# Kernel groups of the lead in order, and late tables moved beside a running convolution

## The chip, the cores and the metric

The kernel runs on one core of a Trainium2 chip. The metric is the device time of one execution in microseconds (us); each kernel is run several times and the median is given. One execution of each kernel is also recorded by the hardware profiler. Its record is "the profile"; answers to questions put to that record are "the trace".

## The reference

The reference filters an input along its length by a state-space convolution and puts a feed-forward network with 4-bit weights on the result. Cut to what matters:

```python
# per head h (64 heads), N = 64 modes, L = 1024 positions, B = 32 sequences
dt  = exp(log_dt);  A = -exp(log_A_real) + 1j * A_imag
Cs  = C * (exp(A * dt) - 1) / A
K   = 2 * Re( sum_n Cs[h, n] * exp(A[h, n] * dt[h] * l) )      # l = 0 .. 1023
y   = causal_convolution(x * mask, K) + D * x * mask           # mask: l < length of the sequence
y   = y * mask
# feed-forward network over the 1024 positions, weights dequantized from 4 bits, groups of 128
gate, up = y @ Wg, y @ Wu                                      # 1024 -> 2752 each
out = x + (silu(gate) * up) @ Wd                               # 2752 -> 1024
```

Each of the 2048 rows (32 sequences x 64 heads) of 1024 positions is one row of the network's input.

## The kernel before

**Blocks.** The 64 heads form four blocks of 16. A block is 16 heads x 32 sequences = 512 columns. The convolution of a block (`conv(blk)`) yields `xh` and `xl`, the high and low float16 halves of the block's network input. There are two such pairs, `c.x[0]` and `c.x[1]`: blocks 0 and 2 use the first, blocks 1 and 3 the second. The network runs on two blocks at a time.

**From parameters to a convolution.** The 64 heads get their convolution kernels in groups of 4 or 8 heads, named by their first head (0, 4, 8, 16, 24, 32, ...). A group passes these steps:

- decay tables: an exponential on ACT (ScalarE), result `xd` (L168 in the lead, L179 in the wide form for two groups);
- phase tables: eight operations on DVE (VectorE), L192 to L204, then sine and square on ACT, L207 and L209 (`phase_tables`, called by `Core.tables`);
- factors `e2` and `e1`: five operations on DVE, L218 to L223 (`kernel_factors`);
- `make_kernel`: small matmuls on PE (TensorE) into the PSUM tile `kq` (L425, L427), its high and low float16 halves `kb` by ACT and DVE (L430, L431), and two stores of `kb` to the DRAM tensor `kpad` (L433). Groups below 24 are stored from ACT's DMA queue, later ones from SP's.
- `toeplitz`: for each head one 512 KB load that reads `kpad` as a 128-row Toeplitz matrix (L525, on SP's queue). Most heads use the three rotating buffers of the tile `t0`, called `t` in the profile; heads of the first block also use borrowed space in `w` and `ihl`.
- `conv_head`: 24 matmuls (L548), eight generator steps of three; after each pair of heads DVE masks the result (`y`, L560), ACT takes the high half `xh` (L563), and GpSimd, or DVE for the last head of a block, the low half `xl` (L565).

The input `u` of four heads is loaded by SP, cast to `uh` by ACT and split into `ul` by DVE (`conv_load`, L503 to L510; `conv_split` in the lead, L495 and L497).

**The lead.** The code from `load_params` to the first network stage handles the parameters (`head_coefficients`, in pieces run by `section`), groups 0, 4 and 8 and conv(0). While conv(0) steps, the table `events` runs extra work at given step numbers (eight steps per head): the kernels of groups 8 and 16, ratios of the scales (`ratios_gu`), a load, and fillers. A filler (`busy`, L891) multiplies two tables into a PSUM tile that nothing reads.

**The network.** `gu_one` and `gu_pair` make gate and up products (L664, L665 and L687, L688) with a rescale of the PSUM tile `chq` after each of eight groups, on DVE (L618, L637) or ACT (L620, L640). `dn_pair` makes the down product for 256 output rows and one block in 22 steps of four matmuls (L736, L737; the last of two, L741), each followed by a rescale on either engine. It ends with a scaled copy `o` (L754 or L758), a residual load `xr` on SP (L775, `residual`), two adds (L762, one on GpSimd and one on DVE) and two stores (L767, GpSimd's queue). The `xr` tile shares a tag with two buffers with `sg`, the output of silu. Weights are unpacked from 4 bits by DVE, GpSimd and ACT (`unpack`, L578 to L599), the down weights `wd` up to and into stage 3.

**The order.** `roll` runs the chains of the network as generators in turn, up to three at a time in the PSUM place "b". Its stages: 0 and 1, single blocks 0 and 1; 2, pairs for blocks 0 and 1; 3 and 4, down products of blocks 0 and 1; 5, pairs for blocks 2 and 3; 6 and 7, their down products. Side work (`sides`) advances by a rate per chain step: in stages 3 and 4 the generator `convs_it` (conv(2), then conv(3)) at `RATES["convs"]`, 1.9 steps. When the first chain of the next stage is opened, what is left of side work marked True is run to its end. The groups 48 and 56 that conv(3) needs are made by `fourth()`, whose scratch space is `c.x[1]` and a pool opened where the unpacking's buffers had been.

Above this, the tile framework orders instructions of each engine by its own planning. `with self.after(key)` gives a key of `self.marks`, an instruction after which the following ones may be placed. Each engine then executes its list in order. SP's list holds DMA issues, and an issue that waits holds those behind it.

Of the kernel before, what the change touches and what calls it, by code (L numbers as in the profile page):

```python
# [32 lines left out]
RATES = {"first": (0.5, 4.6), "fill": (1.0, 0.8), "third": 0.5, "convs": 1.9}  # L33
# [149 lines left out]
def phase_tables(nc, side, pool, co, cst, h0, nh):  # L183
# [20 lines left out]
    stt(r2, r2, off2, pl[:, :, 32:], ALU.subtract, ALU.subtract)  # L204
# [5 lines left out]
    return r1, r2, sq_op  # L210
# [48 lines left out]
class Core:  # L259
    def __init__(self, ctx, tc, io):  # L260
# [15 lines left out]
        self.kpad = self.dram.tile([H, 2, 1152], F16, name="kpad")  # L276
        self.dm, self.known, self.ready = {}, set(), set()
# [127 lines left out]
    def scale_ratios(self, s16, nt, g, name, last_factor):  # L405
# [4 lines left out]
        nc.scalar.copy(s, s16)  # L410
# [32 lines left out]
    def tables(self, pool, h0, nh):  # L443
        held = h0 >= 24
        steps = phase_tables(self.nc, self.nc.vector, pool, self.co, self.cst, h0, nh)
        while True:
            try:
                with self.after("dve" if held else None), self.after("act" if held else None):
                    next(steps)
            except StopIteration as done:  # L450
                self.tab, sq_op = done.value[:2], done.value[2]
                break
            self.dve(800)
            yield
        self.mark(("sq", h0), sq_op)
        self.act(5000)
        yield
        yield from self.pause(5000)
# [33 lines left out]
    def conv_split(self, k, after, last="e"):  # L492
        u, uh, ul = self.us[k]
        with self.after(("sq", after)):
            self.nc.scalar.copy(uh, u)  # L495
        with self.after((last, after)):
            self.nc.vector.tensor_tensor(ul, u, uh, ALU.subtract)  # L497
        self.us[k] = uh, ul
# [219 lines left out]
    def dn_pair(self, k, blk, place):  # L718
# [31 lines left out]
        xr = self.res[k] if blk == 3 else self.residual(self.fw, 2 * k, blk)  # L750
# [21 lines left out]
    def residual(self, pool, n0, blk):  # L772
        rows, cols = slice(128 * n0, 128 * n0 + 256), slice(512 * blk, 512 * blk + 512)
        xr = pool([128, 2, 512], F32) if callable(pool) else pool.tile([128, 2, 512], F32, name="xr", tag="sg", bufs=2)
# [68 lines left out]
def tile_ssm_ffn(ctx, tc, io):  # L843
# [39 lines left out]
    xd = [decay_tables(nc, kg, co, c.cst, h0) for h0 in (0, 8)]  # L883
# [9 lines left out]
    for k, h0 in enumerate((0, 4)):  # L893
        every(c.tables(tables, h0, 4))
# [4 lines left out]
        busy(h0, 8 - 4 * k)  # L899
        c.conv_split(k, h0)  # L900
    every(c.tables(kg, 8, 8))
    every(c.factors(kg, 8, 8, xd[1]))
    c.masks()
# [23 lines left out]
    def kernel_8():  # L927
        c.make_kernel(kg, 8, 8, "b")
        with c.after("act"):
            xd.extend(decay_tables(nc, kg, co, c.cst, h0) for h0 in (16, 24))  # L930
        for k in (2, 3):
            c.conv_split(k, 8, "kb")
# [10 lines left out]
    events = {7: kernel_8, 63: lambda: busy(4, 10), 56: ratios_gu, 87: load_16, 75: lambda: c.make_kernel(kg, 16, 8, "b")}  # L943
    for i, _ in enumerate(c.conv(0)):
        if i in events:
            with c.after("dve" if i == 56 else None):
# [56 lines left out]
    def fourth():  # L1003
        c.forced = True
        every(third_it)
        c.forced = False
        while not c.ready.issuperset(("dn", k, part) for k in range(4) for part in range(3)):
            yield
        c.up_stack.close()
        with tc.tile_pool(name="kg2", bufs=1, side="right") as kg2:  # L1010
            space = c.x[1]
            yield from c.decays(c.scratch(space[:1]), (48, 56))
            c.taps(kg2, 48)
            for h0 in (48, 56):
                yield from c.tables(ScratchPool(c.scratch(space[1:])), h0, 8)
                yield from c.factors(kg2, h0, 8, c.xds[h0])
                for _ in range(3):
                    yield
                c.make_kernel(kg2, h0, 8, "a")
                yield  # L1020
# [3 lines left out]
    def convs():  # L1024
        yield from c.conv(2)
        c.forced = True
        c.need(*(("dn", k, part) for k in range(4) for part in range(3)))
        every(fourth_it)
        c.forced = False
# [97 lines left out]
```

## Time and profile before

| | us |
|---|---|
| median of 3 runs | 1074.47 (1073.33 to 1075.77) |
| the profiled execution's own time | 1075.33 |
| its span in the profile | 1073.5 |
| PE busy | 1026.2 (96%) |
| DVE busy | 803.7 (75%) |
| ACT busy | 775.6 (72%) |
| GpSimd busy | 246.5 (23%) |

Busy shares are means over the whole span. In the row of slices each digit is a fortieth of the span, 26.8 us; PEclk is the clock that the matmul engine was granted, in tenths. In a timeline row the columns are start, duration, engine, line, operation, tiles and count, and in brackets the idle time before it and what ended that. `<-` stands between output and input.

### The profile page before, as it was taken

The numbers are of one execution on the slowest core, as the hardware profiler recorded it, in microseconds if no ns is written. First come the engines' busy times: TensorE is split into PE (matmuls) and PEld (weight loads), VectorE is DVE, ScalarE is ACT, GpSimd is POOL, SyncE is SP. The second block draws the span as 40 slices with busy tenths as digits, with TensorE's granted clock in tenths as the row PEclk, the third lists the DMA queues.
The fourth block names the chain that finished last, engine by engine and source line by source line (L and its number), as shares of the span: only waits on it lengthen the run. The fifth ranks groups of instructions, "written<-read, shape, count | busy, mean of one in ns | idle before, by whom it ended". The sixth has DMA issues, their size and how long they took to land.

```text
span 1073.5 us, 15382 instructions
## 1 busy us (share of the span) xinstructions
PE 1026.2 (96%) x5854; PEld 513.5 (48%) x5854; DVE 803.7 (75%) x939; ACT 775.6 (72%) x1034; POOL 246.5 (23%) x270
## 2 busy tenths in 40 slices
PE   3989999999999999997999999999999999999996
PEld 2867444444344445663665444444444444444442
DVE  8965788888977786768446777777877777777776
ACT  5767777787677777777577777666666667878775
POOL 0333233232332242231103112221111222102102
PEclk9999999999999999999999999999999999999998
DMA  6976321111111534546753001000000001424102
GB/s 197 331 244 211 101 69 40 40 59 40 42 48 50 143 88 156 164 156 196 231 167 128 30 29 51 20 13 17 20 20 20 20 20 58 129 79 148 59 1 79
DMA packets 52099, 99.76 MB, mean 93 GB/s; under 512 B 9524, under 2 KB 11444, under 8 KB 52024
## 3 DMA queue, kind: packets, MB, share of 16 engines
q1 hardware_dynamic: 38888, 70.09, 20.8%
q0 software_dynamic: 5280, 17.31, 4.3%
q10 hardware_dynamic: 7856, 11.37, 3.6%
q8 instruction: 46, 0.75, 0.3%
q14 instruction: 29, 0.24, 0.1%
HBM read 78.99 MB, written 19.76 MB: 92 GB/s over the span
## 4 chain that ended last, share of the span: by engine, by line
PE 83%; ACT 5%; DMA 4%; DVE 4%; issue 2%; POOL 0%; SPq 0%; DVEq 0%; ACTq 0%
PE chq L687 23%; PE chq L688 22%; PE chq L736 13%; PE chq L737 13%; PE cq L548 6%; PE chq L664 2%; PE chq L665 2%; DMA t<-kpad 2%; ACT chq L640 1%; DVE chq L618 1%; ACT chq L620 1%; DVE v L700 1%; DMA ihl<-kpad 1%; DMA ihl<-xF 1%; PE chq L741 1%
## 5 line engine op out<-in xcount | busy, mean ns | idle before, releaser
L687 PE MATMUL chq<-xh,w 128*128 128x512 f16 x1216 | 460.4, 380 | 5.7 <-DVE chq L618 2.1
L688 PE MATMUL chq<-xl,w 128*128 128x512 f16 x1216 | 458.6, 380 | 0.0
L618 DVE TENSOR_SCALAR chq<-chq,gur 128x1024 f32<-128x1024 f32 x261 | 333.2, 1289 | 95.3 <-PE chq L688 94.1
L620 ACT ACTIVATE chq<-chq,gur 128x1024 f32<-128x1024 f32 x285 | 304.3, 1085 | 86.8 <-PE chq L688 85.5
L640 ACT ACTIVATE chq<-chq,dnr 128x512 f32<-128x512 f32 x372 | 242.1, 661 | 71.7 <-PE chq L737 63.8
L736 PE MATMUL chq<-ihl,wd 128*128 128x512 f16 x672 | 253.8, 380 | 6.5 <-ACT chq L640 3.5
L737 PE MATMUL chq<-ihl,wd 128*128 128x512 f16 x672 | 253.4, 380 | 0.0
L637 DVE TENSOR_TENSOR chq<-chq,dnr 128x1024 f32<-128x1024 f32 x129 | 158.4, 1231 | 83.6 <-PE chq L737 83.2
L688 PEld LDWEIGHTS <-w 128*128 128x128 fp8e4 x1216 | 118.9, 98 | 155.3 <-issue 19.4
L687 PEld LDWEIGHTS <-w 128*128 128x128 fp8e4 x1216 | 118.9, 98 | 145.9 <-issue 1.9
L310 POOL TENSOR_TENSOR ihl<-v,ihl 128x512 f16<-128x512 f32 x42 | 48.3, 1150 | 362.9 <-ACT ihl L629 362.9
L737 PEld LDWEIGHTS <-wd 128*128 128x128 fp8e4 x672 | 65.5, 98 | 76.0 <-issue 12.7
L548 PEld LDWEIGHTS <-t 128*128 128x128 f16 x1152 | 81.4, 98 | 39.2 <-DMA t<-kpad 5.9
L736 PEld LDWEIGHTS <-wd 128*128 128x128 fp8e4 x672 | 65.7, 98 | 67.7 <-issue 1.7
L548 PE MATMUL cq<-uh,t 128*128 128x256 f16 (+3 forms) x720 | 91.8, 226 | 4.6 <-DMA t<-kpad 4.5
L565 POOL TENSOR_TENSOR xl<-y,xh 128x512 f16<-128x512 f32 x28 | 36.2, 1294 | 161.5 <-ACT xh L563 161.5
L548 PE MATMUL cq<-ul,t 128*128 128x256 f16 (+3 forms) x360 | 71.6, 225 | 0.0
L629 ACT CAST ihl<-v 128x512 f16<-128x512 f32 x42 | 25.9, 617 | 58.7 <-DVE v L700 55.3
L700 DVE SCALAR_TENSOR_TENSOR v<-chq,gul,sg 128x1024 f32<-128x1024 f32 x38 | 48.6, 1280 | 17.1 <-PE chq L688 11.3
L310 POOL TENSOR_TENSOR spill<-v,spill 128x512 f16<-128x512 f32 x42 | 48.8, 1161 | 14.2 <-ACT spill L629 13.9
L640 ACT ACTIVATE chq<-chq,gur 128x512 f32<-128x512 f32 x66 | 43.2, 661 | 11.0 <-PE chq L665 9.8
L590 POOL TENSOR_TENSOR w<-w,z 128x256 int32<-128x256 int32 x42 | 31.5, 770 | 82.0 <-DVE w L584 77.6
(250 smaller groups left out, 820.5 us busy)
## 6 DMA issues: line engine op xcount, KB each, us to landing
t<-kpad SPq DMA_DIRECT2D x48, 512.0 KB, 4.4
spill<-spill POOLq DMA_DIRECT2D x42, 256.0 KB, 2.7
ihl<-spill ACTq DMA_DIRECT2D x42, 256.0 KB, 2.8
z<-zc SPq DMA_DIRECT2D x29, 256.0 KB, 3.7
u<-xF SPq DMA_DIRECT2D x12, 512.0 KB, 3.7
xr<-xT SPq DMA_DIRECT2D x12, 512.0 KB, 4.7
out<-xr POOLq DMA_DIRECT2D x24, 256.0 KB, 2.9
w<-qgu SPq DMA_DIRECT2D x21, 256.0 KB, 4.1
```

The costliest lines, as they stand in the source:

```text
L310: self.nc.gpsimd.tensor_tensor(out, a, b, op)
L548: nc.tensor.matmul(q[:, d:, h % 2, :], t0[:, lw, 128 * d:128 * d + 128], uu[:, 0:8 - d, h % 4, :], start=(d == 0 and k == 0 and h % 2 == 0 ...
L565: split.tensor_tensor(xl[:, :, ts], yv, xh[:, :, ts], ALU.subtract)
L618: self.mark("dve", self.nc.vector.tensor_scalar(q, q, col, None, ALU.mult))
L620: self.mark("act", self.nc.scalar.activation(q, q, AF.Copy, scale=col))
L637: self.mark("dve", self.nc.vector.tensor_tensor(q, q, cols.to_broadcast([128, 2, 512]), ALU.mult))
L640: self.mark("act", self.nc.scalar.activation(q[:, k], q[:, k], AF.Copy, scale=cols[:, k]))
L687: nc.tensor.matmul(q[:, b], lw, xh[:, g, :], start=(g == 0), stop=False, skip_group_check=True)
L688: nc.tensor.matmul(q[:, b], lw, xl[:, g, :], start=False, stop=(g == GH - 1), skip_group_check=True)
L700: nc.vector.scalar_tensor_tensor(v, q, last, self.sg.pop(ct - 21), ALU.mult, ALU.mult)
L736: nc.tensor.matmul(qs[j], lw, self.ihl[:, g, 0], start=(g == 0), stop=False, skip_group_check=True)
L737: nc.tensor.matmul(qs[j], lw, self.ihl[:, g, 1], start=False, stop=False, skip_group_check=True)
```

## The change

In the lead, groups are put in a fixed order on DVE: the tables of group 4 come after the factors of group 0, those of group 8 after the tables of group 4. The decay tables of heads 8 to 15 come after the squares of group 0. The input splits 0 and 1 come later, and so do the masks. Fillers become 8, 2 and 6 where there were 8, 4 and 10. In conv(0) the kernel of group 8 moves from step 7 to 23, that of group 16 from 75 to 66, and the gate-up scale ratios from 56 to 72.

Late, `fourth()` no longer waits for the unpacking and no longer opens a pool; all of its scratch lies in `c.x[1]`. `convs()` no longer forces it between conv(2) and conv(3): it yields until group 56 is known, and forces `fourth()` only if the side work is itself forced. The rate of `convs` becomes 1.52. The residual tiles of blocks 0 to 2 get a pool `xrp` of two buffers, opened at the end of the first down chain where the unpacking's pool was.

```diff
-RATES = {"first": (0.5, 4.6), "fill": (1.0, 0.8), "third": 0.5, "convs": 1.9}
+RATES = {"first": (0.5, 4.6), "fill": (1.0, 0.8), "third": 0.5, "convs": 1.52}
...
-    def tables(self, pool, h0, nh):
+    def tables(self, pool, h0, nh, key=None):
...
-                with self.after("dve" if held else None), self.after("act" if held else None):
+                with self.after("dve" if held else key), self.after("act" if held else None):
...
+                self.mark(("r", h0), done.value[3])
...
-        nc.scalar.copy(s, s16)
+        with self.after("act"):
+            nc.scalar.copy(s, s16)
...
-        xr = self.res[k] if blk == 3 else self.residual(self.fw, 2 * k, blk)
+        if blk == 3:
+            xr = self.res[k]
+        else:
+            if self.xrp is None:
+                self.need(*(("dn", j, part) for j in range(4) for part in range(3)))
+                self.up_stack.close()
+                self.xrp = self.up_stack.enter_context(self.tc.tile_pool(name="xrp", bufs=2, side="right"))
+            xr = self.residual(self.xrp, 2 * k, blk)
...
-    xd = [decay_tables(nc, kg, co, c.cst, h0) for h0 in (0, 8)]
+    xd = [decay_tables(nc, kg, co, c.cst, 0)]
...
-    for k, h0 in enumerate((0, 4)):
-        every(c.tables(tables, h0, 4))
+    for h0, fillers in ((0, 8), (4, 2)):
+        every(c.tables(tables, h0, 4, ("e", 0)))
+        if h0 == 0:
+            with c.after(("sq", 0)):
+                xd.append(decay_tables(nc, kg, co, c.cst, 8))
         every(c.factors(kg, h0, 4, xd[0][:, h0:h0 + 4]))
         c.make_kernel(kg, h0, 4, "b")
         for h in range(h0, h0 + 4):
             c.t0[h] = c.toeplitz(h)
-        busy(h0, 8 - 4 * k)
-        c.conv_split(k, h0)
-    every(c.tables(kg, 8, 8))
+        busy(h0, fillers)
+    c.conv_split(0, ("sq", 4), ("e", 4))
+    every(c.tables(kg, 8, 8, ("r", 4)))
+    c.conv_split(1, ("sq", 4), ("r", 8))
     every(c.factors(kg, 8, 8, xd[1]))
-    c.masks()
+    with c.after(("e", 8)):
+        c.masks()
...
-    events = {7: kernel_8, 63: lambda: busy(4, 10), 56: ratios_gu, 87: load_16, 75: lambda: c.make_kernel(kg, 16, 8, "b")}
+    events = {23: kernel_8, 63: lambda: busy(4, 6), 72: ratios_gu, 87: load_16, 66: lambda: c.make_kernel(kg, 16, 8, "b")}
...
     def fourth():
-        c.forced = True
-        every(third_it)
-        c.forced = False
-        while not c.ready.issuperset(("dn", k, part) for k in range(4) for part in range(3)):
+        first, second = c.x[1]
+        yield from c.decays(c.scratch([first[:, :4]]), (48, 56))
+        c.taps(ScratchPool(c.scratch([first[:, 4:6]])), 48)
+        for h0 in (48, 56):
+            small = ScratchPool(c.scratch([first[:, 6:8], second[:, 7:8]]))
+            yield from c.tables(ScratchPool(c.scratch([second[:, :7]])), h0, 8)
+            yield from c.factors(small, h0, 8, c.xds[h0])
+            yield from c.pause(c.td - c.tp + HOP)
+            c.make_kernel(small, h0, 8, "a")
             yield
-        c.up_stack.close()
-        with tc.tile_pool(name="kg2", bufs=1, side="right") as kg2:
-            space = c.x[1]
-            yield from c.decays(c.scratch(space[:1]), (48, 56))
-            c.taps(kg2, 48)
-            for h0 in (48, 56):
-                yield from c.tables(ScratchPool(c.scratch(space[1:])), h0, 8)
-                yield from c.factors(kg2, h0, 8, c.xds[h0])
-                for _ in range(3):
-                    yield
-                c.make_kernel(kg2, h0, 8, "a")
-                yield
...
     def convs():
         yield from c.conv(2)
-        c.forced = True
-        c.need(*(("dn", k, part) for k in range(4) for part in range(3)))
-        every(fourth_it)
-        c.forced = False
+        while 56 not in c.known:
+            if c.forced:
+                next(fourth_it)
+            yield
         yield from c.conv(3)
```

More of the change, by code (lines that the diff above doesn't have):

```diff
@@ L203, in phase_tables @@
     stt(r1, r1, off1, pl, ALU.subtract, ALU.subtract)
-    stt(r2, r2, off2, pl[:, :, 32:], ALU.subtract, ALU.subtract)
+    last = stt(r2, r2, off2, pl[:, :, 32:], ALU.subtract, ALU.subtract)
     yield
@@ L209, in phase_tables @@
         sq_op = nc.scalar.activation(r, r, AF.Square, scale=1.4142135623730951)
-    return r1, r2, sq_op
+    return r1, r2, sq_op, last
 def kernel_factors(nc, pool, co, xd, s1, s2, h0, nh):
@@ L276, in __init__ @@
         self.kpad = self.dram.tile([H, 2, 1152], F16, name="kpad")
+        self.xrp = None
         self.dm, self.known, self.ready = {}, set(), set()
@@ L490, in conv_fetch, with conv_split @@
         self.nc.sync.dma_start(self.raw[k][0], self.io["xF"][k])
-    def conv_split(self, k, after, last="e"):
+    def conv_split(self, k, act, dve):
         u, uh, ul = self.us[k]
-        with self.after(("sq", after)):
+        with self.after(act):
             self.nc.scalar.copy(uh, u)
-        with self.after((last, after)):
+        with self.after(dve):
             self.nc.vector.tensor_tensor(ul, u, uh, ALU.subtract)
@@ L773, in residual @@
         rows, cols = slice(128 * n0, 128 * n0 + 256), slice(512 * blk, 512 * blk + 512)
-        xr = pool([128, 2, 512], F32) if callable(pool) else pool.tile([128, 2, 512], F32, name="xr", tag="sg", bufs=2)
+        xr = pool([128, 2, 512], F32) if callable(pool) else pool.tile([128, 2, 512], F32, name="xr")
         self.nc.sync.dma_start(
@@ L928, in kernel_8 @@
         c.make_kernel(kg, 8, 8, "b")
+        for k in (2, 3):
+            c.conv_split(k, "act", ("kb", 8))
         with c.after("act"):
             xd.extend(decay_tables(nc, kg, co, c.cst, h0) for h0 in (16, 24))
-        for k in (2, 3):
-            c.conv_split(k, 8, "kb")
         steps = c.tables(kg, 16, 8)
@@ L941, in load_16 @@
         c.us[4] = c.conv_load(16)
-    events = {7: kernel_8, 63: lambda: busy(4, 10), 56: ratios_gu, 87: load_16, 75: lambda: c.make_kernel(kg, 16, 8, "b")}
+    events = {23: kernel_8, 63: lambda: busy(4, 6), 72: ratios_gu, 87: load_16, 66: lambda: c.make_kernel(kg, 16, 8, "b")}
     for i, _ in enumerate(c.conv(0)):
         if i in events:
-            with c.after("dve" if i == 56 else None):
+            with c.after("dve" if i == 72 else None):
                 events[i]()
```

## The prediction

> **What bounds the kernel now.** I read the page's busy shares and 40 slices first, then tables of engine busy time by stretch, then the timelines of the stretches in which the matmul engine is not full.
>
> ```profile
> PE 1026.2 (96%) x5854; PEld 513.5 (48%) x5854; DVE 803.7 (75%) x939; ACT 775.6 (72%) x1034; POOL 246.5 (23%) x270
> ...
> PE   3989999999999999997999999999999999999996
> ...
> PEclk9999999999999999999999999999999999999998
> ```
>
> TensorE sets the end: 1026 of 1073.5 us. A gain can only come from its idle time, its fillers and its half-clock time. Besides the two ends of the program, the 19th slice (a 7, from 483 us) is the hole. The table by stretch gives both places that the diff touches (columns: length, then busy time and count of PE, PE weight load, DVE, ACT, POOL; last the clock, DMA share, GB/s):
>
> ```profile
> 28.00:30.00 2.00, 1.26 (x20) 1.10 (x21) 1.85 (x4) 1.99 (x7) 0.00 (x0) 0.89 0.18 53
> 30.00:32.00 2.00, 2.00 (x19) 1.88 (x17) 1.44 (x2) 1.95 (x5) 0.00 (x0) 0.50 0.88 215
> 32.00:34.00 2.00, 2.00 (x30) 1.78 (x28) 1.78 (x3) 1.14 (x4) 0.26 (x1) 0.76 1.01 277
> ...
> 490.00:520.00 30.00, 22.14 (x175) 12.47 (x174) 18.50 (x34) 18.10 (x33) 1.15 (x1) 0.94 0.67 211
> 520.00:580.00 60.00, 60.00 (x486) 36.88 (x485) 31.68 (x29) 46.08 (x72) 11.56 (x11) 1.00 0.54 167
> ```
>
> 490 to 520 us: 7.9 us idle. The 3 us stretches inside have clocks 0.86 (495 to 498) and 0.57 (498 to 501): 3 x 0.14 + 3 x 0.43 = 1.7 us more. So 9.6 us lie there. In the lead the clock halves after a gap: 0.2 + 1.0 + 0.5 = 1.7 us. The timelines name the waits:
>
> ```profile
> 17.53 0.63 PE L427 MATMUL kq<-e2t,e1t 128*32 128x32 f32 x8 [13.60 <-DVE e1t L223]
> 18.09 3.78 PE L891 MATMUL wq<-e2t,e1t 128*128 128x128 f32 x16
> ...
> 28.73 0.69 PE L427 MATMUL kq<-e2t,e1t 128*32 128x32 f32 x16 [1.97 <-DVE e1t L223]
> 29.36 12.48 PE L548 MATMUL cq<-ihl,w 128*128 128x256 f16 x168
> 41.69 2.48 PE L891 MATMUL wq<-e2t,e1t 128*128 128x128 f32 x20
> ...
> 60.31 0.28 PE L548 MATMUL cq<-uh,t 128*128 128x256 f16 x1 [1.85 <-DMA t<-kpad]
> ```
>
> The lead is one chain, repeated per group of heads: DVE tables, ACT sine and square, DVE factors, `kq` on PE, `kb` on ACT and DVE, a store to `kpad`, a Toeplitz load, convolution. PE also executes in order, so `kq` of group 8 (28.73) holds seven ready heads behind it.
>
> **The change part by part.**
>
> *Late tables.* Before, `fourth()` waits until all of `wd` is unpacked and is then forced between conv(2) and conv(3): tables, factors, kernels and loads of groups 48 and 56 stand bare. After, it starts in the idle half of `x` with stage 3 and runs beside conv(2); in the built order both `kq` stand among down-projection matmuls with convolutions on both sides, and conv(3) follows without a break. The whole 9.6 us is recovered. No operation is added: two table loads, one wide exponential and two groups of tables as before. Two things are charged back.
>
> (a) Rate 1.9 becomes 1.52 convolution steps per down-projection step. In the built order, before, three quarters of a head remained when the next stage was opened; now 8 heads (192 matmuls, 8 x 1.7 = 13.6 us) stand nearly alone: four heads, 7 others, three heads, 5 others, one head. They live on three `t` buffers.
>
> ```profile
> 510.55 0.28 PE L548 MATMUL cq<-uh,t 128*128 128x256 f16 x1 [1.51 <-DMA t<-kpad]
> ...
> 512.27 14.63 SPq L525 DMA_DIRECT2D t<-kpad  x5
> ...
> 517.04 0.28 PE L548 MATMUL cq<-uh,t 128*128 128x256 f16 x1 [0.84 <-DMA t<-kpad]
> ```
>
> That is the same pattern: head 48 ends at 512.2, its buffer is reloaded at 512.27, head 51 starts at 517.04, a turnaround of 4.8 us. Two other heads cover 3.4. In the new block: heads 56 to 58 are loaded, head 59 waits 1.4 us; the 7 others (7 x 0.216 = 1.5 us) then restore the lead for 60 to 62; head 63 waits about 0.3. At the end stage 5 needs the last head's `y`, `xh`, `xl` (0.2 + 0.69 + 0.62 + 0.69 = 2.2 us) against 4 + 2 + 1 matmuls of cover (1.5 us): 0.7. Sum 2.4; between 0 (loads land early) and 5.
>
> (b) The table work now competes with rescales. The nearest row is the same two-group work of `third()` among the pairs at 228 to 292 us: PE idle in the 4 us stretches there sums to 3.4 us, and the clock fell to 0.69 and 0.88 (1.7 us), so 5.1 us. The pairs have no convolution to fill in; the new order puts 13 to 18 convolution matmuls (about 1 us) where it meets the tables. Bounds 0 and 5.1; I take 2.5, the middle.
>
> Late part: 9.6 - 2.4 - 2.5 = 4.7 us.
>
> *Residual buffers.* `xr` gets two buffers of its own instead of sharing `sg`. SP executes in order: the third and later `xr` loads wait for an earlier store (add, then 2.9 us to land, some 6 us after that chain's last matmul), and `t` loads of heads 57 to 59, 60 to 62 and 63 stand behind such waits in the built order. The chains end about 13, 3 and 2.4 us before the block, so the releases come at about -7, +3 and +4 us on the block's clock; the loads behind could go at 0, 3.4 and 11.4. Cost 0; if a store slips by 3 us, head 60 is late by 2.
>
> *Lead.* Before the first `e1`, DVE no longer has L192, L194, L197, L198, L200, L201, L203, L204 of group 4 and L192 of group 8. By start-to-start that is 0.34 + 0.34 + 0.26 + 0.20 + 0.33 + 0.20 + 0.39 + 0.26 + 0.60 = 2.9 us; part of it filled gaps between dependent coefficient steps (about 0.2 us each when nothing lies between), so I take 2.1: first `kq` at 15.4 instead of 17.5. The rest does not follow. ACT now runs Exp, Sine, Exp, Sine where it ran Exp, Sine: two more table loads, and the second decay table (8 x 0.245 = 2.0 us) stands before `kb` of group 0. Walking the built order with the durations of before: squares of group 0 end 13.1, load and decays 16.4, `kb` 16.7, its store 17.5, sine load 18.8, squares of group 4 at 19.9. DVE has five group-8 steps in front (until 20.3), then factors of group 4 end at 22.3 (before: 20.8). Eight fillers end at 19.8, so PE now waits some 2 us for group 4, then `kq` and two fillers: head 0 at 23.6 instead of 24.5.
>
> Here a rule speaks against the change. The Trainium skill ("ScalarE: Activation LUTs", sections on table sets and the cost of a table load) says to finish one function set before switching and to budget about 2.7 us for each switch, drain included. The row:
>
> ```profile
> 37.91 1.28 ACT L207 ACT_TABLE_LOAD   x1
> 39.20 0.94 ACT L207 ACTIVATE r<-r 128x512 f32<-128x512 f32 x2
> ```
>
> The next activation starts 1.29 us after the load. By the page the two loads would put group 4's factors at about 25 and head 0 at 26.3, 1.8 us later than before; by the row 0.9 earlier. I take the row.
>
> After head 0 the gain is this: `kq` of group 8 now stands behind three heads, so PE no longer waits 1.97 us for it. But the new 2 us gap before group 4 is of the size that halved the clock at 29. The skill ("TensorE: Matmul & The Clock Gate", section on why this matters) allows gaps up to about 3 us. By the page no half clock: 1.7 us more. By the row it returns at 23 to 26. Then `kq` of group 8 comes at 30 to 31, not 28.7, and the loads of group 8 some 1 us later. They were hidden by 2.48 us of fillers at 41.7; six fillers stay. Group 16 gains: its `kb` waited behind two L596 casts (47.20 to 49.28 us), one of which moves behind it (1.1 us). The scale ratios, a mask and two splits move off DVE and ACT at no cost, since the first rescale is at 64.2. So the first head of block 1 (60.31, bound by its load) gains 0.8 with the half clock and 2.0 without. I take 1.3; bounds -1.8 and 3.
>
> *Sum.* 4.7 + 1.3 = 6.0 us. The profiled execution took 1075.33 (span 1073.5, 1.8 around it), which becomes 1069.3; it was 0.86 above the median of the runs, so 1074.47 - 6.0 = 1068.5.
>
> **The rivals.**
>
> *All of it is had* (loads lead, tables hide among convolutions): late part 9.6 - 1.0, lead 2.0, so 1063.9. For it: DMA share at 520 to 580 is 0.54, and PE has convolutions in stage 3. Against: 228 to 292.
>
> *The late part only moves its stall.* With (a) 4 and (b) 5.1 it pays 0.5, lead 1.3: 1072.7. For it: DVE and ACT are already 70 to 75% busy at 405 to 490, with eight unpackings still to come.
>
> *Slower: the block of eight heads starves.* In the lead the same Toeplitz loads landed in 8.2 us at the median, with DMA share above 1.0; at 490 to 610 they landed in 4.4. If the block, where loads go back to back beside `xr` and `spill` loads, takes 8.2, each three heads take 1.7 + 8.2 = 9.9 instead of 5.1: (a) is 8/3 x 4.8 = 12.8 us, and the sum 9.6 - 12.8 - 2.5 + 1.3 = -4.4: 1078.9. It decides from a landing of 6.5 us up. Against: one head per 2.2 us asks for only 240 GB/s, and 417 were seen in the lead.
>
> *It does nothing:* not possible in this built order, since both `kq` and their tables left the stall.
>
> **How the numbers follow.** Likeliest 0.62 (own range 1065.5 to 1071.5), all of it 0.17, moved stall 0.10, slower 0.11. A tenth either way is left out by 1063.5 to 1074.0. This kernel's measurement tells about 0.2% (2.1 us): below 1072.3 is faster. All of the first two and about a third of the moved stall: 0.82; within 0.2%: the rest of it, 0.08; slower 0.10.
>
> **What would show it.** Right: no PE hole near 490 to 520 and no clock below 0.9 there; a run of L548 near 560 to 575 with one or two waits of 1 to 1.5 us on `t<-kpad`; first `kq` near 15.4, a wait on group 4's `e1` of about 2 us, six ACT table loads in the first 40 us, block 1's first head near 59. Wrong: PE holes of over 3 us among the down projections at 410 to 480 (DVE or ACT the bound), `t<-kpad` waits that sum to over 5 us in the late block, or head 0 later than 24.5.

## The result, and the profile after

The changed kernel takes 1085.92 us (median of 4 runs, 1085.24 to 1087.90) against 1075.12 us before (4 runs): a ratio of 1.0109, 95% interval 1.0095 to 1.0123. (Here and below a ratio and its interval come from the single runs, so the ratio can differ by about 0.1% from the quotient of the medians.) It is 10.8 us slower, where 6.0 us faster was forecast, and lies above the forecast range. The profiled execution took 1085.78 us with a span of 1084.0, 10.5 us more than before.

The page of the changed kernel, busy shares and 40 slices:

```profile
PE 1027.6 (95%) x5842; PEld 514.4 (47%) x5842; DVE 812.0 (75%) x943; ACT 771.7 (71%) x1028; POOL 246.5 (23%) x270
...
PE   3989999999899999998997999999999999999996
...
PEclk9999999999999999999998999999999999999999
```

TensorE's work is the same. The 7 at the 19th slice has become an 8, and the 22nd slice, from 569 us, has a 7 now, with a clock digit of 8 under it. Where the old hole lay, 3.2 us of idle time stand now instead of 7.9, and the rows below give them another cause; a second hole opened 85 us later. The table by stretch of the changed kernel (columns as before the prediction):

```profile
490.00:500.00 10.00, 6.84 (x39) 3.44 (x37) 7.67 (x9) 3.50 (x7) 2.76 (x3) 0.83 0.87 280
...
575.00:580.00 5.00, 3.21 (x31) 2.09 (x31) 1.12 (x2) 2.46 (x4) 2.30 (x2) 1.00 0.71 240
580.00:585.00 5.00, 0.59 (x3) 0.44 (x4) 0.00 (x0) 0.00 (x0) 0.00 (x0) 0.56 0.97 281
585.00:590.00 5.00, 5.00 (x61) 4.76 (x59) 0.69 (x1) 0.16 (x1) 0.00 (x0) 0.76 0.62 220
```

From 580 to 585 us no compute engine does anything to speak of, while the DMA share is 0.97. The timelines of PE and then of SP's queue say what is awaited:

```profile
575.07 0.28 PE L551 MATMUL cq<-uh,t 128*128 128x256 f16 x1 [1.38 <-DMA t<-kpad]
...
584.41 0.40 PE L551 MATMUL cq<-uh,t 128*128 128x256 f16 x1 [6.12 <-DMA t<-kpad]
```

```profile
563.13 7.90 SPq L528 DMA_DIRECT2D t<-kpad  x3
576.84 0.37 SPq L785 DMA_DIRECT2D xr<-xT  x1
577.32 2.43 SPq L528 DMA_DIRECT2D t<-kpad  x3
```

Head 59 waits 1.38 us, as forecast (1.4). Head 60 waits 6.12. Its table was issued only at 577.32, directly behind a residual load `xr` that had stood at the head of SP's queue until an older store of `out` landed, and it took 7.1 us to arrive. The other hole, at 490 us, is in DVE's timeline and the next row of PE:

```profile
490.65 0.69 DVE L772 TENSOR_TENSOR xr<-xr,o 128x512 f32<-128x512 f32 x1 [2.22 <-DMA xr<-xT]
491.26 1.64 DVE L200 SCALAR_TENSOR_TENSOR xl<-xl 128x512 f32<-128x512 f32 x1
492.83 0.41 DVE L201 SCALAR_TENSOR_TENSOR xl<-xl 128x256 f32<-128x256 f32 x1
493.16 1.22 DVE L640 TENSOR_TENSOR chq<-chq,dnr 128x1024 f32<-128x1024 f32 x1
```

```profile
494.44 0.38 PE L739 MATMUL chq<-ihl,wd 128*128 128x512 f16 x1 [3.16 <-DVE chq L640]
```

DVE stands 2.22 us for a residual load; behind it come two table steps (1.9 us) and only then the rescale that PE needs.

The lead, PE's timeline after:

```profile
15.43 0.64 PE L429 MATMUL kq<-e2t,e1t 128*32 128x32 f32 x8 [11.54 <-DVE e1t L223]
...
22.42 0.64 PE L429 MATMUL kq<-e2t,e1t 128*32 128x32 f32 x8 [2.07 <-DVE e1t L223]
...
24.00 6.45 PE L551 MATMUL cq<-ihl,w 128*128 128x256 f16 x72
...
30.92 0.69 PE L429 MATMUL kq<-e2t,e1t 128*32 128x32 f32 x16
...
62.48 0.40 PE L551 MATMUL cq<-uh,t 128*128 128x256 f16 x1 [4.93 <-DMA t<-kpad]
```

The first product is at 15.43 (forecast 15.4), the gap before group 4 is 2.07 us (about 2), head 0 starts at 24.00 (23.6; before 24.53). Block 1's first head is at 62.48, 2.2 us later than before. Where the 10.5 us stand, by start of the same matmul in both traces: the first down-projection matmul is 3.1 us later (398.6 against 395.5), the last one 10.6 (1072.9 against 1062.3). So the lead loses 3.1 us, where a gain of 1.3 was forecast, and the late part loses 7.5, where a gain of 4.7 was. (In the seven traces with the old lead that first matmul starts at 393.7 to 396.7 us, in the six with the lead of the change at 397.6 to 399.9: the shift is beyond the scatter, its size good to about 1 us.)

### The profile page after: what moved, and what is told of

The parts are those of the page before. It is cut to its first block, busy times and chain, and to the rows that moved or that the text cites. A ratio compares the mean times of both kernels' runs of the same rounds, so it can differ in the third digit from the quotient of the medians.

```text
span 1084.0 us, 15385 instructions
## 1 busy us (share of the span) xinstructions
PE 1027.6 (95%) x5842; PEld 514.4 (47%) x5842; DVE 812.0 (75%) x943; ACT 771.7 (71%) x1028; POOL 246.5 (23%) x270
## 4 chain that ended last, share of the span: by engine, by line
PE 79%; DVE 7%; DMA 5%; ACT 5%; issue 2%; POOL 1%; DVEq 0%; ACTq 0%; POOLq 0%; SPq 0%
PE chq L690 22%; PE chq L691 22%; PE chq L739 12%; PE chq L740 12%; PE cq L551 6%; DMA t<-kpad 2%; PE chq L667 2%; PE chq L668 2%; ACT chq L643 2%; DMA kpad<-kb 1%; DVE chq L621 1%; DVE v L703 1%; DMA xr<-xT 1%; ACT chq L623 1%; ACT sg L698 1%
## 5 line engine op out<-in xcount | busy, mean ns | idle before, releaser
L643 ACT ACTIVATE chq<-chq,dnr 128x512 f32<-128x512 f32 x362 | 235.3, 661 | 75.1 <-PE chq L740 68.4
L640 DVE TENSOR_TENSOR chq<-chq,dnr 128x1024 f32<-128x1024 f32 x134 | 163.7, 1230 | 74.6 <-PE chq L740 72.7
L311 POOL TENSOR_TENSOR spill<-v,spill 128x512 f16<-128x512 f32 x42 | 48.7, 1160 | 15.5 <-ACT spill L632 15.4
L643 ACT ACTIVATE chq<-chq,gur 128x512 f32<-128x512 f32 x66 | 43.1, 660 | 10.5 <-PE chq L668 9.4
```

What stands on the lines that cost most here:

```text
L311: self.nc.gpsimd.tensor_tensor(out, a, b, op)
L640: self.mark("dve", self.nc.vector.tensor_tensor(q, q, cols.to_broadcast([128, 2, 512]), ALU.mult))
L643: self.mark("act", self.nc.scalar.activation(q[:, k], q[:, k], AF.Copy, scale=cols[:, k]))
```

## The experiments

### The two halves alone

The first run has the late tables, the residual buffers and the rate of 1.52, with the lead of before; the second has the lead of the change, with the late part of before. Against the changed kernel:

```
 # late part alone
-    events = {23: kernel_8, 63: lambda: busy(4, 6), 72: ratios_gu, 87: load_16, 66: ...}
+    events = {7: kernel_8, 63: lambda: busy(4, 10), 56: ratios_gu, 87: load_16, 75: ...}
...
 # lead part alone
-RATES = {..., "convs": 1.52}
+RATES = {..., "convs": 1.9}
...
```

The first also has the old loop over groups 0 and 4, `tables`, `conv_split` and `scale_ratios`, and inputs 2 and 3 are again split behind the decay tables of heads 16 to 31 in `kernel_8`; the second has the old `fourth`, `convs` and `residual`.

> The late part of the change alone: fourth() beside conv(2), rate 1.52, residual buffers of their own; the lead as before. By the traces, the stretch from the first down-projection matmul to the last one took 666.8 us before and 674.3 us after, so if the two parts are independent this kernel is 7.5 us slower than before: 1082.6 us. If the late block stalls only because the lead left the work late or the engines out of step, it is not slower than before (at most 1075), and the tail of conv(3) shows no wait above 2 us on t<-kpad.

Measured: 1081.22 us, ratio 1.0057 (1.0040 to 1.0074).

> The lead's part alone; fourth(), convs and residuals as before. If the parts are independent: slower by the 3.1 us by which the first down-projection matmul came later, 1078.2 us, with block 1's first head at 62.5 us instead of 60.3 and a half-clock stretch after it. If the lead's loss is partly taken up in stages 1 and 2 (their idle time was not the same in the two traces), 1075 to 1077.

Measured: 1078.82 us, ratio 1.0039 (1.0025 to 1.0052). Both halves are slower than before, by 5.9 and 3.5 us, together 9.5 of the 10.8. PE's waits in the late half alone, from 400 to 640 us (total, times, longest):

```profile
PE cq L549 <- DMA t<-kpad: 6.0, 2, 4.7
PE chq L737 <- DVE chq L638: 2.4, 1, 2.4
```

The same two waits as in the whole change (7.5 and 3.9 us there): each half can be studied by itself.

### Cures for the block of eight heads, at the rate of 1.52

The first moves the residual loads of blocks 0 to 2 from SP's to GpSimd's queue, the second gives the tables a fourth buffer, the third does both.

```
-        self.nc.sync.dma_start(xr, ...)
+        self.nc.gpsimd.dma_start(xr, ...)          # first and third
...
-            t0 = self.cv.tile([128, 2, L], F16, name="t0", bufs=3)
+            t0 = self.cv.tile([128, 2, L], F16, name="t0", bufs=4)   # second and third
```

> The changed kernel with one difference: the residual loads xr of blocks 0 to 2 are issued from GpSimd's queue, so that no Toeplitz load stands behind an xr load that waits for a store. Theory A, the blocked queue: the 6.1 us wait of the third last group of heads on t<-kpad falls to under 2 us and the half clock behind it goes, so 6 to 7 us less than the changed kernel: 1079 to 1080 us. Theory B, the block of eight heads on three buffers starves by itself whatever the queue: waits of 1.4 us at every third head remain and the planner has no other matmuls to put between, 1083 to 1085 us.

Measured: 1087.97 us, ratio 1.0117 (1.0100 to 1.0135). Both theories expected a gain, and there is none. SP is free, and still PE starves. The table by stretch:

```profile
575.00:580.00 5.00, 3.96 (x60) 3.79 (x57) 2.67 (x2) 2.27 (x4) 3.39 (x6) 1.00 0.88 240
580.00:585.00 5.00, 2.18 (x39) 2.04 (x36) 0.69 (x1) 0.88 (x2) 0.72 (x1) 1.00 1.01 374
585.00:590.00 5.00, 3.35 (x54) 3.07 (x49) 0.69 (x1) 0.62 (x1) 3.84 (x4) 1.00 0.95 344
```

Two waits of 7.5 us together became four that sum to 6.1 (longest 2.8): with three buffers and a DMA share of 0.88 to 1.01 the heads come at the pace of their loads, which land in 6.5 us at the median.

> The changed kernel with four rotating buffers for the Toeplitz tiles instead of three; residual loads stay on SP's queue. Theory A, the blocked queue: head 60's load now stands in front of the xr load that waited for the store of the first down chain, but those of heads 61 to 63 behind it, so the wait moves by one head and shrinks by about 2 us: 1083 to 1084 us. Theory B, three buffers are too few: the waits in the block go nearly to zero, 1078 to 1080 us.

Measured: 1086.22 us, ratio 1.0106 (1.0091 to 1.0121). No gain, which neither theory had. A fourth buffer moved the stall one head on, as theory A said, but did not shrink it: `t<-kpad` 6.4 us in one wait, since its load stands behind the same residual load (issued at 578.15, the tables at 578.63).

> The whole change at its rate of 1.52, with both cures of the block of eight heads together: residual loads on GpSimd's queue and four table buffers instead of three. Either alone gave nothing (1088.0, 1086.2). Theory Q (each alone was capped by the other: a blocked queue makes buffers useless, and three buffers cap the turnaround): waits on t<-kpad after 550 us under 2 us, 1080 to 1081. Theory D (the block is capped by DMA itself, 0.5 MB for each head of 1.7 us beside residual and spill traffic, at 374 GB/s and a share of 0.9 to 1.0): waits stay at 4 us and more, 1084 to 1088.

Measured: 1082.65 us, ratio 1.0066 (1.0053 to 1.0079): 3.3 us faster than the change. Each cure alone was capped by what the other removes, as theory Q has it, but waits of 2.6 us remain and the whole is 2 us above its forecast. The first hole did not close either, PE's waits:

```profile
PE chq L739 <- DVE chq L640: 4.9, 2, 4.2
PE cq L551 <- DMA t<-kpad: 2.6, 1, 2.6
```

In five runs at this rate DVE's wait for a residual load at 482 to 494 us and PE's longest wait for a rescale behind it go together: 1.34 and 2.4 us (late half alone), 2.22 and 3.2 (the change), 2.86 and 3.9 (four buffers), 3.53 and 4.2 (both cures), 4.03 and 4.8 (GpSimd's queue). PE waits about 0.7 to 1.1 us more than DVE. So most of this hole is the residual load's, whose buffer was not free until the store of an earlier chain had landed; about 1 us is left for the table steps between the add and the rescale. This is read from the five traces; no run at this rate changed the number of residual buffers.

### The rate

One number of the late half alone is changed, then of the whole change, then of the kernel before.

```
-RATES = {..., "convs": 1.52}
+RATES = {..., "convs": 1.9}      # and 2.4, 2.8
```

> The late part of the change alone, with the rate of the convolutions put back from 1.52 to 1.9: 105 convolution matmuls (4.4 heads) instead of 192 (8 heads) are left to stand nearly alone at the end of stage 4, and the third residual load stands in front of the last head's table only. Theory A (what costs the late part its gain is the block that the rate leaves: late tables alone took 1081.2, of which about 6 us of waits on t<-kpad and 2.5 us of lowered clock lie in that block): most of the 8.5 us come back, about 1074 us, with waits on t<-kpad after 550 us that sum to under 3 us. Theory B (the cost is the table work of groups 48 and 56, which delays the rescales of the down projections): it stays at 1080 to 1081, with PE idle time at 400 to 510 us. Theory C (both: the tables' 5 us stay, the block's come back): 1076.

Measured: 1073.00 us, ratio 0.9985 (0.9973 to 0.9997). 8.2 us come back, about what theory A said, though waits on `t<-kpad` are still 5.3 us (three, longest 3.4) and not under 3: the half-sized block still has a stall, but the hole at 490 us is gone (19.59 of 20 us busy from 480 to 500) and no residual load holds DVE.

> As the run before with a rate of 2.4: no block is left, three convolution matmuls stand in front of the next stage. Theory A (the block is the cause): 1071 to 1073, the hole of before (9.6 us at 483 to 505) gone less the tables' cost of 2.5 to 5 us and waits for the convolutions' tables. Theory B: the same 1080 as the run before, since the tables are the same. Theory C: 1074 to 1075. Against A: at this rate a head is due every 20 down-projection matmuls and more, so that tables and rescales of the down projections, now with fewer matmuls between, may hold PE at 430 to 500 us.

Measured: 1066.26 us, ratio 0.9919 (0.9894 to 0.9943), 8.9 us faster than the kernel before (1075.18 beside it). Theory A's 1071 to 1073 was too careful, theories B and C fall: the tables of groups 48 and 56 cost nothing that can be seen. PE's waits from 400 to 640 us and the two critical stretches:

```profile
PE chq L737 <- ACT chq L641: 0.5, 2, 0.3
PE chq L737 <- DMA ihl<-spill: 0.2, 1, 0.2
...
```

```profile
480.00:500.00 20.00, 19.71 (x124) 9.83 (x122) 15.31 (x18) 14.45 (x25) 7.29 (x9) 1.00 0.73 238
...
560.00:580.00 20.00, 19.75 (x134) 10.35 (x132) 13.44 (x13) 14.52 (x23) 6.47 (x7) 1.00 0.46 162
```

No wait for a table is left. From 400 to 600 us PE is idle 1.3 us, where the kernel before has 8.7 and 1.7 more of lowered clock: 7.4 + 1.7 = 9.1, which fits the 8.9 measured.

> The late part with a rate of 2.8. Conv(2) ends earlier, so that in the built order both kernel products of groups 48 and 56 stand among down projections with fewer convolutions (16 matmuls of down projection at a time), and 24 convolution matmuls are left at the end. If only the block matters, as at 2.4: 1066. If convolutions are what covers the tables' rescales, the waits of PE on the rescale lines at 440 to 500 us come back: 1069 to 1073.

Measured: 1066.88 us, ratio 0.9924 (0.9909 to 0.9939), the same within the intervals. The convolutions are not needed as cover for rescales here, and between 2.4 and 2.8 the rate makes no difference that can be seen.

> The whole change, with one number changed: the rate of the convolutions is 2.4 instead of 1.52, so that three convolution matmuls and no block of eight heads are left at the end of stage 4. If the parts add up (late tables with a rate of 2.4 took 1066.3 on their own, the lead part costs 3.6), it takes 1069.8. If the rate is all that is wrong with the change, it takes 1066 or less; if residual buffers or late tables lose time in the whole change for another reason than the block, over 1073.

Measured: 1070.47 us, ratio 0.9957 (0.9943 to 0.9971), as the sum of the parts said (1069.8). The whole change with one number altered is faster than before, and 15.5 us faster than with 1.52. Beyond that sum the late tables and residual buffers lose nothing that can be seen at this rate.

Is it the rate by itself?

> The kernel before with nothing changed but the rate of the convolutions, 1.52 instead of 1.9; the hole at 483 to 505 us and the shared residual buffers stay, and 168 convolution matmuls (7 heads) stand at the end of stage 4. Theory A (the rate is what the late part pays for, whatever the tables): slower than before by the block's waits and lowered clock, 5 to 8.5 us less the 1.5 that before has there: 1079 to 1083. Theory E (the block starves only together with the change's residual loads): within 2 us of before, 1074 to 1077.

Measured: 1079.24 us, ratio 1.0036 (1.0021 to 1.0050). The kernel before, with nothing but the change's rate, is 4.4 us slower, with 5.6 us of waits on `t<-kpad` and without residual buffers of their own. Theory A holds, E falls.

> The kernel before with a rate of 2.4 and nothing else. Theory A says that before has no block to lose, and the hole of 9.6 us between the convolutions stays: 1073 to 1077. If the gain of the late part at 2.4 (to 1066.3) came from the rate alone: 1066 to 1068.

Measured: 1082.14 us, ratio 1.0069 (1.0054 to 1.0084), slower than either theory allowed. A high rate in the old structure uses up conv(2) sooner (its last matmul is at 475.6 us, before 486.1) and leaves the bare table block alone. The stretches of this run:

```profile
480.00:500.00 20.00, 14.26 (x70) 5.48 (x69) 16.93 (x31) 13.83 (x25) 5.54 (x6) 0.74 0.43 139
500.00:520.00 20.00, 18.18 (x197) 13.44 (x195) 8.91 (x9) 9.64 (x16) 6.21 (x6) 1.00 0.90 312
```

The hole is 5.7 us idle with a clock of 0.74 here (20 x 0.26 = 5.2 us more). From 400 to 640 us idle time and lowered clock sum to 17.8 us, before to 10.4: the 7.3 us of the medians. So the gain needs both: the late part at the old rate gains 2.2 us, the rate of 2.4 without it loses 7.3, and together they gain 8.9. No run separates the late tables from the residual buffers that came with them.

### The lead

The lead part alone, with one thing put back or moved in each run: ten filler steps instead of six before head 8; group 8's kernels after two heads or one instead of three; the scale ratios at step 24 instead of 72.

```
-    events = {23: kernel_8, 63: lambda: busy(4, 6), 72: ratios_gu, ...}
+    events = {23: kernel_8, 63: lambda: busy(4, 10), 72: ratios_gu, ...}
+    events = {15: kernel_8, 63: lambda: busy(4, 6), 72: ratios_gu, ...}
+    events = {7: kernel_8, 63: lambda: busy(4, 6), 72: ratios_gu, ...}
+    events = {23: kernel_8, 63: lambda: busy(4, 6), 24: ratios_gu, ...}
+    events = {7: kernel_8, 63: lambda: busy(4, 6), 24: ratios_gu, ...}
```

> The lead part of the change alone, with ten filler steps instead of six in front of head 8. With six, PE waited 2.67 us there (40.2 to 42.85), and the clock was at half speed from 44 to 48 us: 2.0 x 0.4 + 2.0 x 0.45 = 1.7 us of work, after which the kernel product of group 16 came at 48.69 instead of 47.23. Theory L1 (the fillers that were taken away cost the lead part its gain through that half clock): the wait shrinks to about 1.8 us, the clock stays at 1.0, the product of group 16 comes 1.5 us earlier, block 1's first head at about 60.4 instead of 61.95, and the kernel takes 1076.5 to 1077.5. Theory L2 (group 16 is set by its own kb behind the unpacking of weights, and the first head of block 1 by DMA): first head stays at 61.9, 1078.8.

Measured: 1077.84 us, ratio 1.0022 (1.0013 to 1.0031). 1.0 us comes back at the median, with intervals that overlap, and not as theory L1 said: PE still waited 2.43 us for head 8 and the clock was halved for longer.

> The lead part alone, with the kernels of group 8 made after two heads instead of three (before: one). In the lead part alone e1 of group 8 is ready at 27.2 us, 1.5 us earlier than before, but its product stands at 30.32 behind the third head. Theory L3 (the late product of group 8 costs the lead part its gain: everything behind it, the loads for head 8, the tables of 16, is late by the same): product at about 28.7, loads for head 8 issued at 37.2 instead of 38.85, wait before head 8 about 1 us and no half clock, first head of block 1 at 60 to 60.3, 1076 us. Theory L2 (group 16's kb waits behind weights): the loads for head 8 come earlier, block 1's first head stays within 0.5 us of 61.95, 1078 to 1079.

Measured: 1079.20 us, ratio 1.0033 (1.0018 to 1.0048). L3 falls. The product came 1 us earlier, but the stores of `kb` were issued 0.6 us earlier and landed 6.8 us later, and head 8's loads went out at 39.40, not at 37.2.

> The lead part alone, with the kernels of group 8 made after one head (as before the change); e1 of group 8 is ready at 27.2. Making them after two heads gave nothing, because the stores of kb were issued only 0.6 us earlier (30.87) and landed 6.8 us later, as in the lead part alone (7.2), where before they took 4.5. Theory L4 (the stores stand in the DMA engines behind the loads that SP issued before them: of the four Toeplitz loads of heads 4 to 7, which the lead part issues 1.5 us earlier, then the block 1 input and a weight tile; the loads for head 8 can start only when the stores have landed, and the DMA engines have nothing in between, share 0.03 to 0.1 at 38 to 40 us): with the product at about 28 the stores go out at about 29 and land by 34.5, the loads for head 8 start by 36, no stretch of 2 us between 34 and 46 has a DMA share under 0.5, PE waits under 1 us for head 8, first head of block 1 by 60.3, 1075 to 1076. Theory L5 (the loss of the lead part comes from group 16 alone, whose kb stands behind unpacked weights on ACT and behind tables on DVE): the loads for head 8 come earlier, block 1's first head stays at 61.5 to 62.5, 1078 to 1079.

Measured: 1080.22 us, ratio 1.0036 (1.0022 to 1.0050). The loads follow theory L4 to the letter, and the time does not: they start at 35.98 and block 1's first head at 58.55, 1.8 us before the old kernel's. PE's timeline and the DVE column (third pair) of its stretches:

```profile
58.55 0.28 PE L550 MATMUL cq<-uh,t 128*128 128x256 f16 x1 [0.85 <-DMA t<-kpad]
...
63.98 0.38 PE L666 MATMUL chq<-xh,w 128*128 128x512 f16 x1 [3.14 <-ACT xh L565]
```

```profile
40.00:50.00 10.00, 7.44 (x93) 6.30 (x92) 6.14 (x10) 6.55 (x15) 3.10 (x3) 0.83 1.05 389
50.00:62.00 12.00, 9.68 (x148) 9.08 (x145) 12.00 (x18) 3.45 (x5) 5.39 (x5) 1.00 0.82 260
```

DVE has no free moment from 50 to 62 us, and `xh` waits for it (and at the end for 0.7 us of other work on ACT). Before, the same stretches have:

```profile
40.00:50.00 10.00, 10.00 (x146) 9.25 (x144) 9.45 (x15) 6.53 (x10) 5.67 (x6) 1.00 1.04 363
50.00:62.00 12.00, 9.30 (x138) 8.80 (x136) 10.65 (x19) 6.96 (x11) 7.39 (x6) 1.00 0.78 247
```

The change moved the scale ratios (some 3.6 us of DVE) from step 56 to step 72, out of a stretch where DVE now idles 3 to 6 us into one where it is full.

> The lead part alone, with the scale ratios of the gate and up projections made at step 24 of block 0 instead of step 72, so that their 3.6 us of DVE work stand before kb of group 16 and not behind it (before: step 56, in DVE's gaps at 39.5 to 49.2). Theory L6 (DVE work put off to the end of the lead is what the lead part loses: DVE idles 5.5 us at 40 to 50 and is full from 50 to 62): gains 1 to 2.5, 1076.5 to 1078. Against: in this run the output multiplication of head 8, which waits for PE, stands in front of the reciprocals, and so they may push kb of group 16 back by up to 2.5 us: then 1079 to 1081, and the run with the early product tells more.

Measured: 1082.60 us, ratio 1.0059 (1.0042 to 1.0077), worse, and above even the 1079 to 1081 of the objection in the expectation. Its mechanism is in the trace: a mask and four reciprocals stand in front of DVE's half of group 16's `kb`, which comes at 54.70 us instead of 51.80 in the lead alone.

> Both: the kernels of group 8 after one head, and the ratios at step 24, where they fall into DVE's idle time at 43 to 49 us. With the early product alone block 1's first head came at 58.55, the first gate-up matmul at 63.98 after a wait of 3.14 us for xh, and it took 1080.2. Theory L6: DVE has 3 us less to do from 50 to 62, the wait for xh falls below 1 us, first gate-up matmul by 61.5, 1075 to 1076.5, that is the whole loss of 3.6 or more comes back. Theory L7 (what follows block 1's first head is set by weights on POOL and ACT, or by lost time at 145 to 150 us where a store of spill lands late): the wait for xh stays above 2 us or the loss reappears at 145 us, 1078 to 1080.

Measured: 1078.62 us, ratio 1.0027 (1.0017 to 1.0038), in the range of theory L7.

> The run before, and the kernels of group 8 made after one head, as before the change, instead of after three. Theory L4 below: 1065 to 1067.5. Theory L5: 1069 to 1070.

Measured: 1071.01 us, ratio 0.9958 (0.9946 to 0.9970): no gain over 1070.47.

> The whole change at the rate of 2.4 with both repairs of the lead. Theory L6: the 1071.0 of the run without the ratios moved falls by 3 to 4.5, to 1066.5 to 1068. Theory L7: 1070 to 1071.

Measured: 1071.14 us, ratio 0.9950 (0.9931 to 0.9969): none either, although its first gate-up matmul is at 61.86 us, against 66.33 in the run of 1070.47 us. Landmarks of the runs of the lead, from their timelines and stretches (us):

| run | product of group 8 | head 8's loads issued | block 1's first head | first gate-up matmul | last one of the single blocks | DVE busy 40 to 50, 50 to 62 |
|---|---|---|---|---|---|---|
| before | 28.73 | 37.22 | 60.31 | 62.15 | 160.02 | 9.45, 10.65 |
| after | 30.92 | 39.59 | 62.48 | 65.96 | 164.42 | 6.64, 11.75 |
| lead alone | 30.32 | 38.85 | 61.95 | 65.41 | 164.44 | 4.50, 12.00 |
| ten fillers | 30.20 | 39.38 | 62.27 | 65.02 | 162.84 | 2.88, 10.91 |
| group 8 after two heads | 29.36 | 39.40 | 62.96 | 65.38 | 164.25 | 3.83, 11.31 |
| group 8 after one | 27.23 | 35.98 | 58.55 | 63.98 | 166.07 | 6.14, 12.00 |
| ratios at 24 | 30.29 | 39.41 | 62.86 | 65.62 | 169.85 | 4.98, 11.51 |
| group 8 after one, ratios at 24 | 28.03 | 38.25 | 59.99 | 62.60 | 162.83 | 9.29, 10.00 |

The last row shows that theory L6 holds as far as 62 us: with DVE's work back in its old place the first gate-up matmul is at 62.60, 0.45 us behind the old kernel. Then the loss returns, in PE's timeline of that run:

```profile
71.06 0.61 PE L426 MATMUL kq<-ihl,cst 1*32 1x256 f32 x2
74.87 0.69 PE L428 MATMUL kq<-e2t,e1t 128*32 128x32 f32 x16 [2.41 <-DVE e1t L223]
```

Now the product of group 24 waits, because on DVE a split that stood 1.69 us for ACT was ahead of its factors. A second loss, also in the lead alone and in the whole change, lies at 145 to 150 us (PE busy 3.00 and 3.25 of 5, before 5.00): ACT waits 1.81 and 1.46 us there for an older `spill` store. Why that store landed later than before, and how much of the 3.5 us it makes, was not tested.

The ratios at 24 alone gave nothing (65.62), since in the change the first gate-up matmul is held by another chain, that of group 16. DVE's half of its `kb` and the loads for block 1 that wait for its stores, first before, then in the change:

```profile
49.68 0.41 DVE L431 SCALAR_TENSOR_TENSOR kb<-kq,kb 32x256 f16<-32x256 f32 x1 [0.51 <-ACT kb L430]
...
56.03 1.40 SPq L525 DMA_DIRECT2D t<-kpad  x3
```

```profile
51.14 0.41 DVE L433 SCALAR_TENSOR_TENSOR kb<-kq,kb 32x256 f16<-32x256 f32 x1
...
58.30 1.64 SPq L528 DMA_DIRECT2D t<-kpad  x3
```

The loads go out 2.3 us later, block 1's first head starts 2.2 us later after a wait of 4.93 us, and behind that wait the clock is 0.50, 0.50 and 0.67 for three us (1.3 us lost): 3.5 of the 3.8 us by which the first gate-up matmul is late. Only when these loads come early (54.22 us with group 8 after one head) is the work put off on DVE what is waited for. So up to 62 us the traces show two things, each of which holds that matmul by itself: the late chain of groups 8 and 16, and DVE work put off to 50 to 62 us. No run gave the whole loss back as time, and what an order without the later stalls would give stays open.

### A version that beats both

It is the late part with a rate of 2.4 (1066.26 us) and the lead of before: late tables, residual buffers and the rate, and no other edit.

## Why the prediction was wrong, by its steps

- **The hole recovered (9.6).** Right: at a rate of 2.4 the late tables gained 8.9 us.
- **Term (a), the block of eight heads: 2.4, bounds 0 and 5.** This is the main step that failed. In the change, PE is idle 7.8 us at 560 to 600 us, and the clock of 0.76 at 585 to 590 takes another 1.2 and its neighbour some 0.2: 9.2 us. The first wait was forecast exactly (1.38 against 1.4). The mistake was to read the turnaround of 4.8 us in conv(3), where loads go out one at a time, as that of three loads back to back; the first of these landed 7.1 us after issue, where head 59's, issued alone at 570.67, took 4.4. With 4.4 us head 60 would have waited 3.4 us for its late issue alone, an estimate from these rows; the slower landing makes the other 2.7. The rate that makes the block was taken as given and priced as a remainder, although it was the one number of the diff that could be changed without touching anything else. The runs price it at 8.2 us from 1.52 to 1.9 and 15.0 to 2.4.
- **Residual buffers: "Cost 0; if a store slips by 3 us, head 60 is late by 2".** Failed. Head 60's buffer was free at 572.2, its load went out at 577.32. The release forecast for +3 us on the block's clock came at +7.9, since two adds on GpSimd took 3.23 us, the stores behind them went out from 570.92 us on, and stores of `out` took 5.2 us at the median to land there, not 2.9; the head was late by 6.1. The step missed that the same buffers also hold DVE at 490 us, where the load is waited for by an add that stands ahead of rescales.
- **Term (b), tables against rescales: 2.5, bounds 0 and 5.1.** The hole it spoke of cost 3.9 us idle and 1.7 of clock (0.66 from 495 to 500), with 1.4 more idle than before at 400 to 480: 7.0. But the cause named was wrong for most of it: the residual load has all but about 1 us of the hole, and of the 1.4 us the kernel before at a rate of 1.52, without late tables, has 1.1 as well. At 2.4 the same tables beside the same rescales cost nothing; the pairs at 228 to 292 us (where the idle time sums to 3.5 us, not 3.4) were no model for it.
- **The lead: +1.3, bounds -1.8 and 3.** It was -3.1. The walk to head 0 was right to 0.4 us, the step behind it was not: group 8's loads were 2.4 us later and not 1, because its stores of `kb` went out 1.5 us later and took 6.8 us to land where they had taken 4.5. "Group 16 gains" (1.1 us) failed: DVE's half of its `kb`, now behind table steps of the next group, came 1.5 us later and its loads 2.3, so that block 1's first head was at 62.48 and not near 59, with the half clock behind it. And "the scale ratios, a mask and two splits move off DVE and ACT at no cost, since the first rescale is at 64.2" failed: the reader of the ratios was watched, not the engine they moved to. DVE was full there (11.75 of 12 us), which cost 3.14 us of waiting for `xh` as soon as the loads came early.
- **Sum.** 9.6 - 9.2 - 7.0 - 3.1 = -9.7, against -10.8 measured and -10.5 between the two profiled executions.
- **The rival on the other side** named the right place and sign (the block starves, 1078.9), with landings of 8.2 us as the mechanism. The landing was 7.1 for head 60 and 6.9 at the median from 576 to 590 us, over its point of decision of 6.5; it lacked the queue, the other hole and the lead.
- **The two rules of the Trainium skill.** "ScalarE: Activation LUTs" (section on the cost of a table load) would have put head 0 at 26.3; the two new loads took 1.28 us each (at 12.92 and 17.42, the next activations at 14.21 and 18.72) and head 0 came at 24.00, so the row was right. "TensorE: Matmul & The Clock Gate" (section on why this matters) allows gaps up to about 3 us; in the change the gap of 2.07 us left the clock at 1.00, as the page says, but in the lead alone the same gap of 2.07 us was followed by 0.50 at 24 to 26 us. Neither the row of before nor the page settles it; a gap of 2.78 us without a lowered clock speaks for the page, one of 1.72 us with it against (more in the last section).

## What to carry to other kernels

A rate that spreads cover work over a stage is part of the cost of every edit in that stage: ask what it leaves at the stage's end, and try two other values before anything is concluded about the edit. A load that waits for a buffer stands in front of all later loads of its queue and, through its reader, in front of all later work of that engine; price it at both places, with loads that land back to back. When work is moved away from an engine's idle time, look at how full the engine is where it lands, not only at when its result is read.

## What was not expected of the hardware

The half clock has no fixed threshold in the length of a gap here. Over all 20 traces, from 20 us on, the shortest gap of PE after which the granted clock fell to 0.5 within 4 us, with no longer gap near it, was 1.36 us (at 44.42, the whole change at 2.4 with both repairs of the lead), the longest after which it stayed at 1.00 was 3.34 us (at 61.57, the kernel before at 1.52). Between them both happen: at one and the same matmul a gap of 2.07 us left the clock at 1.00 in the change and was followed by 0.50 in the lead alone. Of 18 gaps of 3.0 to 6.4 us 17 were followed by a lowered clock; the 11.5 us before the very first product were not. A gap is the idle time in front of one matmul; small matmuls near it, such as those that make `kq`, count as work here, and what they do to the clock was not tested.

Two stores of 16 KB, `kpad<-kb`, took 4.5 us at the median before, 5.1 with group 8 after one head, and 6.8 to 7.2 in the lead alone and with group 8 after two heads, where more of SP's 512 KB loads had been issued ahead of them; no run changed these loads alone. At the end of it the DMA engines of the lead alone were nearly idle, a share of 0.10 from 38 to 40 us, since the next loads waited for those stores:

```profile
38.00:40.00 2.00, 2.00 (x29) 1.99 (x26) 1.69 (x4) 1.98 (x8) 1.23 (x2) 1.00 0.10 16
```
